# Loads issued by ScalarE, a planner that counts the DMA engines, and the last residual on GpSimd alone, in a four-layer graph network kernel

## The chip, the core and the metric

The kernel runs on one core of a Trainium2 chip. A core has a matrix engine (TensorE, PE in the profile, with its weight loads as PEld), a vector engine (VectorE, DVE), an activation engine (ScalarE, ACT), GpSimd (POOL) and a fifth sequencer, SyncE (SP), that only issues transfers here. Each of them works through its own instruction stream in order and waits for the others by semaphores. Transfers are issued by an instruction of one of these streams, and are then carried out by 16 DMA engines. The metric is the device time of one execution in microseconds (us); shorter is better.

## What is computed

For 128 graphs of 128 nodes with 256 features each, four layers run one after the other. Each normalises the features of a node, takes the ReLU, runs a graph layer, and adds the result to x:

```python
h = jnp.maximum(_layernorm(x, axis=-1), 0.0)
# layer 0: gated graph network, L = 3 steps with their own weight[i] and one common GRU cell
A = (adj != 0).astype(x.dtype)
for i in range(L):
    m = jnp.einsum('bnd,de->bne', h, weight[i])
    aggr = jnp.einsum('bst,bsd->btd', A, m)
    gi = aggr @ w_ih.T + b_ih
    gh = h @ w_hh.T + b_hh
    i_r, i_z, i_n = jnp.split(gi, 3, axis=-1)
    h_r, h_z, h_n = jnp.split(gh, 3, axis=-1)
    r, z = sigmoid(i_r + h_r), sigmoid(i_z + h_z)
    n = jnp.tanh(i_n + r * h_n)
    h = (1.0 - z) * n + z * h
x = x + h
...
# layer 1: y = sum over relations r = 1..4 of (adj == r) @ h @ weight[r], plus a bias
# layers 2 and 3: graph attention, softmax over the neighbours of e = leaky(s1_i + s2_j), then alpha @ (h W)
```

All data are float32. The adjacency matrix holds only 0 and 1, so three of the four relations of layer 1 are empty.

## The kernel before

**Tiling.** The graphs are cut into NG = 32 groups of G = 4 graphs. All buffers are preallocated: three tiles `xs` for x, five `adjs` for adjacency matrices, 24 `form`, 11 `big`, three `wide`, eight PSUM banks. A group passes through load, norm, three GRU steps (`step`), layer 1 (`neighbours`), the two attentions (`attention`, `attend`) and a store. Up to `AHEAD = 5` groups are in work at a time, so that TensorE always has products of one group while another waits.

**Three-pass products.** A float32 operand is split into parts of the type fp32r: `hi` (a rounding, line 955 or 957), `lo` (line 961) and `df`, a difference of the two (`difference`, line 470). The product then takes three passes of TensorE with a rescaling of the PSUM bank between the second and the third (`rescale`, line 1013; `scale` at line 830 in layers 1 and 2). The GRU products are line 992. In layers 1 and 2 the same splitting is used (`THIN = (1, 2)`, lines 806 to 834, product line 819), except in the last `PLAIN = 2` groups; layer 3 uses plain float32 products (line 775). Both kernels have these constants.

**Transposes.** `turn` (line 478) transposes a tile of 128x512 without TensorE: a block transpose on VectorE (line 490), a "give" that writes it to a `swap` tile in HBM (line 493), and a "take" of four transfers that reads it back in another order (line 502). After each GRU step the new h comes back this way. After the last step it is added to x (`residual`, lines 1078 to 1083), by VectorE or GpSimd as the planner finds it best.

**Loads.** `fetch` reads x in two transfers of 256 KB, twice for each group (`x0` for layer 0 and again `x1` for the residual, because there are only three `xs` tiles); `load`, `again` and the transfer at line 1095 read the adjacency matrix, again, and transposed. That is seven loads for each group, all issued by SP, in the same stream as the gives, the takes, two small transfers of each attention (lines 1151 and 1153) and the stores (line 1220).

**The order.** No engine's order is written by hand. `Plan.op` collects operations with a cost in ns, their engine (or a choice of two) and the buffers that they read and write. `Plan.order` (line 215) then plays the operations on a model of the engines while the kernel is built: it ranks each operation by the length of what follows it, by its group times `PERIOD`, and by an entry of the table `OFFSETS` (a number for each place in the code and stage of the run), and always places the operation that can start first. `LAG` and `HOP` are the delays with which one engine sees another's result. A transfer is an operation of 470 ns on SP, and its result is seen 4500 ns later (`LAG["SP"]`), changed by `late` (`GIVE`, `TAKE`, `LINE`, `SPREAD`). An operation with `port=True` does not overlap another such one on VectorE or GpSimd in the model (line 349). On the chip only the resulting order counts: every instruction waits for its semaphores, whenever the model thought that they would come.

**The branch.** The program holds two versions of most of the run, one for adjacency matrices with relations above 1. With these inputs the first is taken, and all counts below are of it.

Of the kernel before, what the change touches and what calls it, by code (L numbers as in the profile page):

```python
# [10 lines left out]
I32 = mybir.dt.int32  # L11
# [7 lines left out]
P = 128  # L19
D = 256  # L20
KC = D // P
G = 4
# [12 lines left out]
LAG = {"PE": 165, "ACT": 110, "DVE": 85, "POOL": 20, "SP": 4500, "ACTQ": 2500}  # L35
# [3 lines left out]
OWN = {"PE": 0, "ACT": 125, "DVE": 125, "POOL": 80, "SP": 2500, "ACTQ": 2500}  # L39
PERIOD = 29902  # L40
CLOSE = 7183
CLOSING = 2
SOON = -210
# [3 lines left out]
LINE, SPREAD = 0, -1000  # L47
GIVE = -400
TAKE = -2500
TENSOR = ()  # L50
BLOCK = 32
NEAR = 69
# [20 lines left out]
def seen(o, h):  # L73
    return o.late + (LAG[o.eng] + HOP[h.eng] if h.engs != (o.eng,) else OWN[o.eng])


def act(n, ptrs=0):
    return 50 + 95 * ptrs + 0.833 * n


def dve(n):
    return 68 + n / 0.96


def dma(kb):
    return 470
# [3 lines left out]
    0: (-70252, -12514, 2287, 8809, -26238, -146194, 10750, 55634, 30994, -54821, -2879, -215, -254,),  # L90
    1: (-77596, -18751, -40109, -33244, -13055, -53723, -68528, 1773, -34806, -135119, 879, -98768, 51856,
        44795, -64452, -2716,),
    2: (-95804, -20611, 70568, -66959, -6282, -38365, 6331, 7167, -87557, -120685, 144159, 0, -60172, 22200,
        253, 2907, 38047,),
    3: (-102445, -23990, 38859, 16506, -38395, -77755, 61821, 576, 58832, 37279, 38392, 48590, -137270, -161,
        -4329, 88294, -5659, -1511, -24936, -35483,),
    4: (9420, 6970, 96990, 45577, 14137, -3081, -28597, -108133, -850, -77398, -8748, -81, 24213, -39147,
        5274, -117520, -39070, 4328, 73461, 2677, -9322, 38218,),
    5: (-53063, -10484, 13614, 9709, -9223, 0, 86360, -49387, 3891, -79089, 22834, -12125, 42, -143071,
        -20815, -7001, 39402, 8197, 210921, 979, -8129, 55104, -109511, 178418, -171023, -17919, -45955,  # L100
        32785, 202299, 15929, -75290, -16189,),
    6: (-8401, 1876, 0, -2867, -17545, -54409, -177384, 6635, -4173, 16809, 64025, 1422, -41374, 3498, 7298,
        112681, -960, 0, -167733, 3047, -20901, 48681, -50794, 104147, -14530,),
    7: (2011, -43268, -7473, -2193, -13120, 17374, 10030, 24727, -8835, -59753, 29500, -32772, -10542,
        -85496, -6214, -47593, 4322, -5746, -43839, -101654, -3101, 9392, -18883,),
    10: (31340, 140410, 166041, 86764, 86271, -82403, 47762, 173067, 157481, -33091, 90840, -8460, 85813,),
    11: (-90811, -5747, -11338, -10756, 2168, -27498, -36330, -9110, 13623, -65824, 59954, -36485, 65854,
        102114, -39462, 10659,),
    12: (-88894, -2718, 120398, -47746, 16864, -33143, 17060, 25017, -58235, -111482, 170409, 89873, -65258,
        61044, 3422, 23111, 49690,),  # L110
    13: (-59071, 17894, 109447, 41927, -4268, -51312, 111328, 77067, 108356, 88471, 46360, 263340, -35253,
        23414, 79162, 211888, 10834, -10383, 74698, 67176,),
    14: (-32758, 12684, 122607, -43352, -20519, -34186, -56784, -88737, -18648, -122741, -24236, -29303,
        31876, -49287, -17477, -128202, -71886, 71670, 64769, 11212, -103569, -34527,),
    15: (-186417, -106904, -40789, -64266, -8033, -13445, 16411, -115394, -129609, -221523, -34547, -153159,
        -40482, -146129, -99541, -93701, -50044, 14115, 99121, -155460, -34394, 49772, -135635, 90451,
        -238640, -50117, -75732, -67304, 110359, -120923, -153053, -106347,),
    16: (90192, 31519, 28924, 59971, 13927, -108659, -126696, 35607, 7022, 44259, 134646, 83504, 72967,
        -71833, 139898, 214088, -4475, 66727, -178916, 46932, 84371, 67621, 13000, 119832, 93548,),
    17: (2011, -43268, -7473, -2193, -13120, 17374, 10030, 24727, -8835, -59753, 29500, -32772, -10542,  # L120
        -85496, -6214, -47593, 4322, -5746, -43839, -101654, -3101, 9392, -18883,),
    20: (-107741, -75380, -118420, -44708, -69924, -229335, -95079, 10513, -7484, 27055, -96949, -215, -254,),
    21: (-241039, -37443, -85617, -204164, -130954, -212658, -180409, -165567, -39823, -261311, -133885,
        -103620, -20641, -66103, -225402, -138454,),
    22: (-120431, -90137, 129948, -127092, 11177, -90000, -80347, -35815, -106293, -139261, 141530, -54256,
        -129233, 7860, -119111, 29072, 3576,),
    23: (-144176, -87227, -85789, 1378, -81324, -238467, -3162, -78700, 46997, -3871, 33809, 42358, -177604,
        -35904, -119077, -63937, -38348, -135903, -24936, -35483,),
    24: (-200969, -199448, -70412, -199813, -160146, -250664, -235592, -342997, -205357, -303708, -186137,
        -202706, -168399, -243146, -236370, -300082, -270699, -214705, -104544, 2677, -9322, 38218,),  # L130
    25: (-61251, -50204, -55609, -84828, -90010, 10545, -51986, -177143, -111208, -144284, 59013, -46623,
        -56779, -179794, -83802, -190091, -64080, -63359, 54466, -41363, -72589, -54011, -140205, 135055,
        -306980, -77123, -140787, 32785, 202299, 15929, -75290, -16189,),
    26: (-81589, -13318, 8156, -109205, -83353, -110277, -231535, -35494, -89897, 10694, 20288, -77730,
        -166910, -72981, -43136, 895, -48027, -102602, -242066, -114463, -91143, 43689, -72571, 104147,
        -14530,),
    27: (2011, -43268, -7473, -2193, -13120, 17374, 10030, 24727, -8835, -59753, 29500, -32772, -10542,
        -85496, -6214, -47593, 4322, -5746, -43839, -101654, -3101, 9392, -18883,),
# [19 lines left out]
class Op:  # L158
    __slots__ = ("engs", "eng", "times", "ns", "fn", "deps", "heirs", "bufs", "group", "key", "port", "rush", "late", "rank", "wait", "ready", "end", "most", "tag")
# [12 lines left out]
class Plan:  # L172
    def __init__(self):
        self.ops = []
        self.group = 0
        self.shared = True
        self.keys = 0
        self.most = 0
        self.stage, self.sites = 7, {}

    def op(self, eng, ns, fn, r=(), w=(), after=(), port=None, rush=0, late=0):

        o = Op(*((eng, ns) if isinstance(eng, tuple) else ((eng,), (ns,))), fn, self.group)
        o.port = eng == "POOL" if port is None else port
        o.rush, o.late, o.most = rush, late, self.most
        if self.shared:
            o.key = self.keys  # L190
            self.keys += 1
# [1093 lines left out]
```

## Time and profile before

| what | value |
|---|---|
| time, median of 3 runs | 2342.71 us (2341.92 to 2347.65) |
| the profiled execution | 2353.06 us, of which the profile's span is 2351.2 us |
| granted TensorE clock | 0.996 of full speed on average |
| GRU products, line 992 | 6912 matmuls of 128x512, of 12137 matmuls in all |
| differences on GpSimd, line 470 | 383 of `form` (mean 1362 ns) and 120 of `cform` (mean 1294 ns) |
| residual, line 1080 | 47 on VectorE (mean 870 ns), 13 on GpSimd (mean 1315 ns) |
| rescaling, line 1013 | 448 on ScalarE (mean 574 ns); on VectorE 128 (line 1011, mean 695 ns) |
| moved over DMA | 270.36 MB, mean 115 GB/s; nearly all of it on queue q1, that of SP |

The span is the time from the first to the last instruction that the profile saw; what is left of the execution's own time, 1.9 us, lies around it. The busy time of TensorE counts matmuls that overlap in its pipeline with modelled ends, so 97% does not mean that nothing could be gained beside the remaining 3%: the distance from start to start of two GRU matmuls in an undisturbed row is 0.229 us (11.92 us for 52 of them in the chain of waits). "Idle before" in a row is idle time of that engine alone.

### The profile page before, as it was taken

Reading aid. Unit: us, or ns where it says so; the run is one execution under the profiler, and the core shown is the slowest. Engines: PE = TensorE matmul, PEld = TensorE weight load, DVE = VectorE, ACT = ScalarE, POOL = GpSimd, SP = SyncE. Lnnn points to the kernel's source line nnn. Section 1 sums busy time; section 2 is a strip of 40 time slices with the busy share of each in tenths; the row PEclk is TensorE's granted clock in tenths of the full one; section 3 lists DMA queues with packets and bytes.
Section 4 is the critical chain, followed back from the end, with each engine's and each line's share of the span. In section 5 each row is a group of like instructions: output and inputs, shape, how many; then the busy total and the mean of one; then the engine's idle time right before and its main releaser. Section 6 shows DMA issues by size and latency. Waiting matters only on the chain.

```text
span 2351.2 us, 39064 instructions
## 1 busy us (share of the span) xinstructions
PE 2291.9 (97%) x12137; PEld 1947.2 (83%) x12137; DVE 1978.2 (84%) x5405; ACT 1582.0 (67%) x3272; POOL 912.4 (39%) x729
## 2 busy tenths in 40 slices
PE   7999999999999999999999999999999999999997
PEld 6788888888888888888888888888888888788885
DVE  7858888888888888888888888888888888888887
ACT  6566676766676666666666766666766666666665
POOL 2334334443334443334343334343334343344421
PEclk9999999999999999999999999999999999999999
DMA  8535445555445455455455455455554555545431
GB/s 249 143 83 110 96 90 124 117 128 116 102 110 125 111 133 113 100 117 117 114 126 118 107 115 115 114 129 116 108 115 112 118 122 109 128 103 118 105 77 43
DMA packets 951273, 270.36 MB, mean 115 GB/s; under 512 B 677008, under 2 KB 939280, under 8 KB 951056
## 3 DMA queue, kind: packets, MB, share of 16 engines
q1 hardware_dynamic: 949968, 266.72, 50.0%
q8 instruction: 99, 1.62, 0.3%
q14 instruction: 118, 0.97, 0.2%
q10 hardware_dynamic: 1088, 1.05, 0.1%
HBM read 168.96 MB, written 98.69 MB: 114 GB/s over the span
## 4 chain that ended last, share of the span: by engine, by line
PE 64%; DVE 14%; DMA 10%; ACT 6%; SPq 4%; issue 3%; DVEq 0%; POOL 0%; ACTq 0%
PE bank L992 40%; PE bank L819 7%; PE bank L765 6%; PE bank L974 5%; PE bank L775 5%; DMA swap<-big 4%; SPq L502 4%; DMA big<-swap 3%; DVE junk L1119 3%; DVE form L961 2%; DMA wide<-swap 2%; ACT big L743 1%; DVE wide L1042 1%; DVE wide L1045 1%; DVE big L490 1%
## 5 line engine op out<-in xcount | busy, mean ns | idle before, releaser
L992 PE MATMUL bank<-form,wh_s 128*128 128x512 f32 x3456 | 953.4, 396 | 8.7 <-ACT bank L1005 4.6
L992 PE MATMUL bank<-form,wi_s 128*128 128x512 f32 x3456 | 944.0, 393 | 1.6 <-ACT bank L1013 0.9
L470 POOL TENSOR_TENSOR form<-form,form 128x512 fp32r<-128x512 f32 x383 | 517.7, 1362 | 800.4 <-DVE form L961 565.0
L992 PEld LDWEIGHTS bank<-form,wi_s 128*128 128x128 f32 x3456 | 644.1, 188 | 143.6 <-ACT bank L1013 3.1
L992 PEld LDWEIGHTS bank<-form,wh_s 128*128 128x128 f32 x3456 | 631.8, 188 | 151.5 <-ACT bank L1005 15.8
L1013 ACT ACTIVATE bank<-bank 128x512 f32<-128x512 f32 x448 | 255.4, 574 | 325.7 <-PE bank L992 324.4
L722 POOL TENSOR_TENSOR small<-small,nhalf 128x4 f32<-128x4 f32 (+2 forms) x140 | 142.2, 1020 | 408.8 <-DVE small L720 338.9
L1119 DVE CUSTOM_DVE_ANT_0 junk<-big,ub 128x256 bf16<-128x256 f32 x512 | 244.5, 478 | 14.2 <-ACT big L743 0.5
L743 ACT ACTIVATE big<-xs,small 128x256 f32<-128x256 f32 x384 | 200.1, 590 | 21.6 <-DVE small L726 12.2
L696 DVE BATCH_NORM_STATS2 small<-xs 128x6 f32<-128x256 f32 x512 | 190.0, 415 | 7.3 <-DMA xs<-in_x_dram 6.0
L470 POOL TENSOR_TENSOR cform<-cform,cform 128x512 fp32r<-128x512 f32 x120 | 155.2, 1294 | 96.2 <-DVE cform L811 83.0
L490 DVE STREAM_TRANSPOSE big<-wide 128x512 f32<-128x512 f32 x252 | 173.1, 697 | 4.0 <-ACT wide L743 2.3
L1035 DVE SCALAR_TENSOR_TENSOR bank<-big,bank 128x512 f32<-128x512 f32 x192 | 131.9, 690 | 48.5 <-PE bank L992 35.9
L955 ACT ACTIVATE form<-wide 128x512 fp32r<-128x512 f32 x179 | 109.2, 626 | 83.7 <-DMA wide<-swap 43.4
L1179 ACT ACTIVATE big<-big,small 128x128 f32<-128x128 f32 x256 | 99.8, 392 | 70.0 <-DVE small L1173 69.7
L1023 ACT ACTIVATE bank<-bank,b_rz 128x512 f32<-128x512 f32 x192 | 123.4, 655 | 34.0 <-PE bank L992 30.1
L1210 DVE SCALAR_TENSOR_TENSOR xs<-bank,small,xs 128x256 f32<-128x256 f32 x256 | 118.4, 475 | 31.6 <-PE bank L775 23.0
L1042 DVE TENSOR_TENSOR wide<-wide,bank 128x512 f32<-128x512 f32 x192 | 126.9, 682 | 21.4 <-ACT bank L1040 21.1
L765 PE MATMUL bank<-big,big 128*128 128x128 f32 x1024 | 130.7, 277 | 11.9 <-DVE wide L1045 7.1
L1023 ACT ACTIVATE big<-bank,b_rz 128x512 f32<-128x512 f32 x192 | 130.1, 681 | 16.3 <-PE bank L992 12.1
L765 PEld LDWEIGHTS bank<-big,big 128*128 128x128 f32 x1024 | 123.1, 192 | 19.4 <-DVE wide L1045 9.9
L974 PE MATMUL bank<-adjs,big 128*128 128x128 f32 x1024 | 131.2, 276 | 6.4 <-DMA big<-swap 5.1
(105 smaller groups left out, 3297.5 us busy)
## 6 DMA issues: line engine op xcount, KB each, us to landing
swap<-big SPq DMA_DIRECT2D x312, 256.0 KB, 2.5
big<-swap SPq DMA_DIRECT2D x992, 64.0 KB, 2.3
xs<-in_x_dram SPq DMA_DIRECT2D x128, 256.0 KB, 3.1
adjs<-in_adj_dram SPq DMA_DIRECT2D x64, 256.0 KB, 3.4
wide<-swap SPq DMA_DIRECT2D x128, 128.0 KB, 3.6
big<-line SPq DMA_DIRECT2D x60, 256.0 KB, 3.9
out_dram<-xs SPq DMA_DIRECT2D x30, 512.0 KB, 3.1
big<-in_adj_dram SPq DMA_DIRECT2D x32, 256.0 KB, 4.0
```

The lines of the kernel that those rows point to most:

```text
L470: (nc.gpsimd if eng == "POOL" else nc.vector).tensor_tensor(at(df), at(lo).bitcast(F32), at(hi).bitcast(F32), ALU.subtract)
L490: nc.vector.transpose(part.t, src())
L696: op("DVE", dve(D), lambda g=g: nc.vector.bn_stats(s.t[:, ST + 6 * g : ST + 6 * g + 6], xt.t[:, g, :]), r=[(xt, {g})], w=[(s, {("mv", g)})])
L743: nc.scalar.activation(place(g), xt.t[:, g, :].rearrange("p (k m) -> p k m", k=KC), AF.Relu, bias=s.t[:, MR + g : MR + g + 1], scale=s.t[: ...
L765: nc.tensor.matmul(ps.t[:, (len(gs) * k + j) * P : (len(gs) * k + j + 1) * P], hs[g // 2].t[:, (g % 2) * D + k * P : (g % 2) * D + (k + 1) ...
L819: nc.tensor.matmul(po.t[:, j * D : (j + 1) * D], fs[f].t[:, (len(gs) * k + j) * P : (len(gs) * k + j + 1) * P], w.t[:, f, k, :], start=(st ...
L974: nc.tensor.matmul(pg.t[:, g * P : (g + 1) * P], of()[:, g * P : (g + 1) * P], flags(m0)[:, g * P : (g + 1) * P], start=True, stop=True,)
L992: nc.tensor.matmul(ps.t, w.t[(slice(None), *row, j, k, slice(c * P, (c + 1) * P))], b.t, start=(start and x == 0), stop=(x == len(terms) - ...
L1013: nc.scalar.mul(ps.t, ps.t, by)
L1023: op("ACT", act(T, 1), lambda: nc.scalar.activation(to.t, ps.t, AF.Tanh, bias=b_rz.t[:, c : c + 1], scale=0.5), r=[b_rz, *([ps] if kept el ...
L1042: op("DVE", dve(T), lambda c=c, ps=ps: nc.vector.tensor_tensor(hT.t[:, c, :], hT.t[:, c, :], ps.t, ALU.subtract), r=[ps], w=[(hT, {c})])
L1119: nc.vector.tensor_tensor_reduce(out=junk.t, in0=part, in1=ub[i].t[:, v, :], op0=ALU.mult, op1=ALU.add, scale=1.0, scalar=0.0, accum_out=s ...
```

## The change

1. **The seven loads of each group go from SP's stream to ScalarE's.** A new function `arrive` issues them with `nc.scalar.dma_start` when `QUEUE` is "ACT". The weights, gives, takes, stores and the small transfers stay where they were.
2. **The planner counts the DMA engines.** A transfer gets a length `moves`. In `place` a running time `engines` is pushed on by each transfer, and the result is seen at its end plus `LAND` = 1400 ns plus `late`, in place of a fixed 4500 ns; `GIVE` and `TAKE` are 0, and a load on ScalarE's queue has `late` = 4700. An issue costs 530 ns.
3. **GpSimd and VectorE may overlap by `EASE` = 400 ns in the planner's model of their port,** and a few costs of operations are a little larger (`act`, `dve`, the attention terms 880 for 850).
4. **The residual of the last step runs on GpSimd alone.**
5. **All of `OFFSETS`, and `PERIOD`, `CLOSE`, `SOON` and `NEAR`, have new values,** so the order of every engine is new.

```diff
-LAG = {"PE": 165, "ACT": 110, "DVE": 85, "POOL": 20, "SP": 4500, "ACTQ": 2500}
+LAG = {"PE": 165, "ACT": 110, "DVE": 85, "POOL": 20, "SP": 0, "ACTQ": 0}
...
-OWN = {"PE": 0, "ACT": 125, "DVE": 125, "POOL": 80, "SP": 2500, "ACTQ": 2500}
-PERIOD = 29902
-CLOSE = 7183
+OWN = {"PE": 0, "ACT": 125, "DVE": 125, "POOL": 80, "SP": 0, "ACTQ": 0}
+PERIOD = 30728
+CLOSE = 21788
...
-SOON = -210
+SOON = -2537
...
-LINE, SPREAD = 0, -1000
-GIVE = -400
-TAKE = -2500
+LAND = 1400
+LINE, SPREAD = 1300, 100
+GIVE = 0
+TAKE = 0
...
+ISSUE = 530
+EASE = 400
+LANDING = 4700
+ARRIVAL = 2300
+QUEUE = "ACT"
...
-NEAR = 69
+NEAR = 41
...
 def seen(o, h):
-    return o.late + (LAG[o.eng] + HOP[h.eng] if h.engs != (o.eng,) else OWN[o.eng])
+    return (o.late + LAND + o.dma if o.dma is not None else 0) + (LAG[o.eng] + HOP[h.eng] if h.engs != (o.eng,) else OWN[o.eng])
...
+            o.seen = end
+            if o.dma is not None:
+                n = P // BLOCK if o.ns == ISSUE * P // BLOCK else 1
+                engines = max(max(engines, end - (n - 1) * ISSUE) + o.dma, end + o.dma / n)
+                o.seen = engines + LAND + o.late
             if o.port and eng != "ACT":
-                port = max(port, end)
+                port = max(port, end - (EASE if eng == "POOL" else 0))
...
+        def arrive(dst, src, w, after=()):
+            on_act = QUEUE == "ACT"
+            op(QUEUE, dma(256), lambda: (nc.scalar if on_act else nc.sync).dma_start(out=dst(), in_=src), w=w,
+               after=after, late=LANDING if on_act else ARRIVAL, moves=800)
+
         def fetch(gi, name, after=()):
             xt = Buf(xs, f"{name}{gi}")
             for g2 in range(G // 2):
-                op("SP", dma(256), lambda g2=g2: nc.sync.dma_start(
-                    out=xt.t[:, 2 * g2 : 2 * g2 + 2, :],
-                    in_=x[ds(gi * G + 2 * g2, 2)].rearrange("g n d -> n g d")),
-                   w=[(xt, {2 * g2, 2 * g2 + 1})], after=after)
+                arrive(lambda g2=g2: xt.t[:, 2 * g2 : 2 * g2 + 2, :],
+                       x[ds(gi * G + 2 * g2, 2)].rearrange("g n d -> n g d"), [(xt, {2 * g2, 2 * g2 + 1})], after)
...
                 for k, h in enumerate(hs_new if i == L - 1 else ()):
-                    def residual(eng, k=k, h=h):
+                    def residual(k=k, h=h):
                         part = xt.t[:, :, k * P : (k + 1) * P]
-                        (nc.gpsimd if eng == "POOL" else nc.vector).tensor_tensor(
-                            part, part, h.t.rearrange("p (g d) -> p g d", g=G), ALU.add)
-
-                    op(("DVE", "POOL"), (dve(T), 1250), residual, r=[h], w=[(xt, set(range(G)))], port=True)
+                        nc.gpsimd.tensor_tensor(part, part, h.t.rearrange("p (g d) -> p g d", g=G), ALU.add)
+
+                    op("POOL", 1250, residual, r=[h], w=[(xt, set(range(G)))], port=True)
```

## The prediction

> **What bounds the kernel now.** I read the busy shares, then windows of the run, then who made TensorE wait, then the waits on the engines that the change touches.
>
> ```profile
> PE 2291.9 (97%) x12137; PEld 1947.2 (83%) x12137; DVE 1978.2 (84%) x5405; ACT 1582.0 (67%) x3272; POOL 912.4 (39%) x729
> ```
>
> TensorE is busy for all but 59 us. Windows (length, then busy PE, PEld, DVE, ACT, POOL) say where those are:
>
> ```profile
> 0.00:60.00 60.00, 44.82 (x181) 36.36 (x182) 43.11 (x116) 37.42 (x101) 14.68 (x18) 0.91 0.88 248
> ...
> 1000.00:1400.00 400.00, 398.32 (x2140) 341.33 (x2139) 345.32 (x929) 272.61 (x551) 161.27 (x126) 1.00 0.51 116
> ...
> 2300.00:2351.20 51.20, 36.33 (x187) 28.73 (x185) 38.62 (x222) 27.61 (x84) 11.39 (x18) 0.91 0.17 49
> ```
>
> 15.2 us lie in the first 60 and 14.9 in the last 51; between them only 29 us are idle in 2240. VectorE, at 345.3 of 400, is the next engine. What held TensorE up (total, times, longest):
>
> ```profile
> PE bank L765 <- DVE wide L1045: 7.1, 12, 1.5
> PE bank L598 <- DMA big<-in_wihT_dram: 6.3, 1, 6.3
> PE bank L765 <- ACT big L743: 5.3, 1, 5.3
> PE bank L974 <- DMA big<-swap: 5.1, 8, 1.5
> ...
> PE bank L992 <- ACT bank L1005: 4.6, 7, 1.0
> PE bank L765 <- DMA big<-swap: 3.9, 6, 1.6
> ```
>
> So it is TensorE's own work plus many small stalls. Counted over the executed branch, TensorE has the same 10271 instructions in both programs, three-pass products included: their part of the change's name is no change here. Between start and end only stalls can be gained. If every idle microsecond in the middle went (29) and the ends stayed, the profiled execution would take about 2324 us; that is nearly the floor.
>
> **1. The residual leaves VectorE.** It waits in order for a take to land:
>
> ```profile
> DVE xs L1080 <- DMA big<-swap: 66.5, 45, 3.3
> ```
>
> 47 adds of 870 ns are 41 us of VectorE's work, and 69.6 us of its idle time precede them. What stands behind waits too: at 342.6 us VectorE has waited 2.1 us for the take, and TensorE's next GRU products start 0.34 us late, released by ScalarE's L1005. All seven stalls "L992 <- L1005" (4.6 us) come within 6 us of such a residual; with smaller ones of the same cause I take **-6 us** (ends: 0, if the new order has its own such waits, and -12). On GpSimd the 47 adds cost 47 x 1.315 = 62 us, and the wait stands there before differences and the norm's power. GpSimd has 1439 idle us. The new order also takes 95 differences (63 `form`, 32 `cform`) off it.
>
> **2. VectorE and ScalarE get other work.** Counts of both orders times the rows: VectorE gains 96 x 0.67 (differences; one row has it at 674 ns) + 28 x 0.68 + 40 x 0.68 + 26 x 0.42 (roundings) = 121 us, and loses 41 (residual) + 76 x 0.695 = 53 (rescalings): net +27 us, from 84% to 85%. ScalarE gains 76 x 0.574 = 44 us and loses 28 x 0.595 + 40 x 0.597 + 26 x 0.626 = 57. All this lies beside TensorE's work. A difference on VectorE takes half of GpSimd's 1362 ns, which shortens the way to the third pass; 27 us more on the second-fullest engine leaves less room. I take **0** (ends -10 and +27, all of it uncovered).
>
> **3. The loads leave SP.** There are 224. SP waited with them at its head:
>
> ```profile
> SPq L513 <- ACT wide L743: 120.6, 54, 8.9
> SPq L513 <- DMA out_dram<-xs: 69.9, 25, 4.4
> ```
>
> 190 us in which gives and takes queued behind could not be issued. The Trainium skill speaks against an effect: in "DMA: Bandwidth & Descriptors", section "Issuing engines are not separate DMA queues", all issuers' transfers interleave on the same 16 DMA engines, and a second issuer saves only the sequencer's time. By that rule I would count 224 x 0.47 us of SP's time, which bounds nothing: 0. The rows show more than issue time, a wait in the queue, with late takes as 9.0 us of TensorE's stalls (L974 and L765 above). I take the rows, less one: **-8 us** (ends 0 and -9).
>
> **4. ScalarE issues them.** One issue takes it about 0.5 us (three in 1.57 us at the start), so 224 take 112 us, and ScalarE goes from 67% to about 72%. Behind each issue stand tanh, exponentials and rescalings that free PSUM banks. In the new order 16 loads stand right before a rescaling, and 43 right before a gate's tanh. Moreover every transfer of the program waits until the one issued eight before it has landed (eight semaphores in turn), whichever queue it is on. In steady state, for one of seven loads in a group, the second half of x0, the eighth before is a take only about 2.8 us of TensorE work earlier; a take needs up to four issues and 2.3 us, so ScalarE may stand 0 to 1.5 us there. ScalarE has about 23 idle us in a group's 71, and the order leaves over 3 us of TensorE work, by the matmuls in between, before a GRU product that depends on it. I take **0** in the steady part (ends 0 and +36; see the second rival).
>
> **5. The start.** The eight-transfer limit is visible before:
>
> ```profile
> 0.73 0.48 ACTq L542 DMA_DIRECT2D big<-in_w0T_dram  x1
> ...
> 2.24 4.30 SPq L513 DMA_DIRECT2D xs<-in_x_dram  x4
> 2.84 1.28 ACT L580 ACT_TABLE_LOAD   x1 [2.84 <-issue]
> ```
>
> SP issues four loads and ScalarE four; then SP stands until first ones land, while ScalarE is free from 2.8 us and splits its first weights at 8.38. In the new program 13 transfers (nine loads of x and adjacency, four of weights) stand before ScalarE's first activation. The last of them is the 23rd transfer of all, and before the 23rd was issued at 14.40 us. So ScalarE begins some 5 us later. Weights `whh` come earlier in exchange (first on SP), and ScalarE has some 14 idle us between 8 and 60 to catch up. I take **+4 us** (ends 0 and +6).
>
> **6. The end.** After the last GRU product both orders have the same 35.3 us of TensorE work by the planner's costs, in 62 operations, and no loads: **0** (ends -4 and +4). The planner's new accounting costs nothing at run time; what it does is in the order.
>
> **Sum:** -6 + 0 - 8 + 0 + 4 + 0 = -10 us on the profiled 2353.06 (span 2351.2 plus 1.9), 2343.1, a ratio of 0.9958. On the median of 2342.71 that is **2333 us**, some 0.4% faster.
>
> **The rivals.**
> - *No change.* TensorE is full, the late takes and the VectorE waits were covered but for 4.6 + 9 us, and a new order has new places with thin cover, as the old one has (L765 behind L1045 recurs in many groups). Gains and the start cancel: 2343 us. For it: 398.3 busy of 400 in the best window leaves little. Against: other windows are worse (394.8 from 600 to 1000).
> - *Slower: ScalarE is held by its loads.* Place: load issues and their waits in ScalarE's stream, ahead of rescalings. Price: 7 x 0.5 + about 1.3 of waiting = 4.8 us in a group. It decides once ScalarE is so late that TensorE has used up its cover; with a quarter reaching TensorE, 1.2 us x 30 groups = 36, plus 4, less the 14 gained: +26 us, 2379 profiled, **2369 us**. For it: the order was planned without the eight-transfer limit, and a load that waits for a store or a reader now blocks ScalarE and not SP. Against: a third of ScalarE is idle.
> - *Slower: VectorE becomes the bound.* 27 us more, uncovered, less part 3 and plus part 5: 27 - 8 + 4 = +23 us, **2366 us**. Against: 85% is not full, and the residual's waits go.
>
> **Chances.** The forecast 0.45 (own range 2310 to 2336), no change 0.23, ScalarE held 0.22, VectorE 0.10. A measurement of this kernel tells 0.3% (7 us) from nothing: faster 0.45, same 0.23, slower 0.32. The range, with the unknown ends in it: low 2308 (the cited gains at their far ends, -12 - 10 - 9 - 4 = -35), high 2372 for the two slower cases.
>
> **What would show it.** Right: L1080 gone from VectorE's waits, no L513 row among SP's, fewer stalls of L974 and L765 for takes, ScalarE's first activation near 13 us, TensorE's middle windows above 99%. Wrong: rows in which ScalarE's DMA issues wait long and L992 waits for L1013 or L1005 in every group; VectorE above 88% in the middle windows; GpSimd's residual wait delaying L992 through L470.

## The result, and the profile after

The changed kernel takes 2500.53 us (median of 4, 2498.53 to 2504.74), beside 2343.34 us for the kernel before on the same chip (2341.92 to 2347.65): a ratio of 1.0668 [1.065, 1.0685], 157 us slower, where 2333 us and a gain of 0.4% were forecast. In the new program the lines stand 14 to 16 lower: the GRU products are L1008, their rescaling on ScalarE L1029, the aggregation L990, the residual L1096, the loads L527.

The same three views of the changed kernel's profile as were read before: busy time and share, windows, and who made TensorE wait (total, times, longest).

```profile
PE 2335.9 (93%) x12137; PEld 1959.4 (78%) x12137; DVE 2119.0 (85%) x5472; ACT 1569.4 (63%) x3253; POOL 855.8 (34%) x681
```

```profile
0.00:60.00 60.00, 35.30 (x152) 28.76 (x153) 40.60 (x110) 32.53 (x90) 10.61 (x14) 1.00 0.79 230
1000.00:1400.00 400.00, 377.33 (x1973) 316.12 (x1972) 346.38 (x882) 253.72 (x523) 140.59 (x109) 0.99 0.48 109
2440.00:2502.90 62.90, 48.43 (x225) 38.72 (x224) 44.34 (x244) 31.00 (x97) 10.76 (x18) 0.83 0.14 40
```

```profile
PE bank L990 <- DMA big<-swap: 51.7, 23, 3.8
PE bank L835 <- ACT bank L846: 34.3, 30, 1.8
PE bank L1008 <- ACT bank L1029: 16.8, 19, 1.8
```

TensorE has the same 12137 matmuls. It idles 167.0 us of the span (2502.9 less 2335.9) in place of 59.3, and its busy time, whose ends are modelled, is 44.0 us longer, at a granted clock of 0.986 in place of 0.996. The loss is not at the ends: the window in the middle has 22.7 us of idle TensorE in 400, where before it had 1.7. And it is not that another engine is full: VectorE is at 346.4 of 400 (345.3 before), ScalarE at 253.7 (272.6). All work more slowly together.

What is new among the waits of the other engines, in three answers for ScalarE, VectorE and GpSimd:

```profile
ACT adjs L870 <- DMA adjs<-in_adjT_dram: 68.0, 30, 3.2
ACT adjs L865 <- DMA adjs<-in_adj_dram: 58.2, 32, 4.3
...
DVE small L712 <- DMA xs<-in_x_dram: 66.0, 50, 4.9
...
DVE adjs L948 <- DMA adjs<-in_adj_dram: 21.5, 25, 1.0
...
POOL xs L1096 <- DMA big<-swap: 156.5, 23, 10.1
```

ScalarE stands 126.2 us at loads of adjacency and VectorE 87.5 at loads. (L865, L870 and L948 convert a loaded adjacency matrix from int32, L712 takes the statistics of a loaded x; they are the first users of their loads.) Before, the same answers have 2.1 and 7.7 us, mostly these:

```profile
ACT adjs L849 <- DMA adjs<-in_adj_dram: 1.9, 2, 1.0
...
DVE small L696 <- DMA xs<-in_x_dram: 6.0, 3, 4.3
```

One such place, in the timeline of ScalarE (start, duration, instruction; in brackets the idle time before it):

```profile
1206.14 0.66 ACT L1021 ACTIVATE bank<-bank,b_hn 128x512 f32<-128x512 f32 x1
1207.00 0.60 ACT L822 ACTIVATE cform<-bank 128x512 fp32r<-128x512 f32 x1 [0.20 <-PE bank L781]
1207.01 0.37 ACTq L527 DMA_DIRECT2D adjs<-in_adjT_dram  x1
1209.83 0.62 ACT L870 CAST adjs<-adjs 128x512 f32<-128x512 int32 x1 [2.23 <-DMA adjs<-in_adjT_dram]
1210.35 0.66 ACT L1021 ACTIVATE bank<-bank,b_hn 128x512 f32<-128x512 f32 x1
```

ScalarE issues the load at 1207.01 and the very next instruction of its stream uses it, at 1209.83; the rescalings and gates behind that wait as well. In the changed order this is so for 56 of the 64 adjacency loads that ScalarE converts. Why does the planner put the user there? In `Plan.op` of the changed kernel, line 197, only an operation whose engine is called SP or ACTQ is a transfer:

```
o.dma = (300 if moves is None else moves) if o.engs[0] in ("SP", "ACTQ") else None
```

`arrive` makes the load an operation of "ACT". So its `dma` is None, `place` lets its result be seen at the end of the issue, and `late`, `LAND` and `moves` are never used: the 4700 ns of `LANDING`, listed above as part of the change, are dead text. On the chip a load lands 2.9 to 4.2 us after its issue (medians; last column of the page's transfers; 2.9 is that of adjT):

```profile
swap<-big SPq DMA_DIRECT2D x312, 256.0 KB, 2.8
big<-swap SPq DMA_DIRECT2D x992, 64.0 KB, 2.4
xs<-in_x_dram ACTq DMA_DIRECT2D x128, 256.0 KB, 4.2
adjs<-in_adj_dram ACTq DMA_DIRECT2D x64, 256.0 KB, 3.0
```

In the old order a median of 5.0 to 9.2 us of TensorE work, by the planner's costs, stand between a load and its first user, in the new one 0.9 to 1.4. (The second x, x1, had 23.8 and has 4.6.)

### The profile page after: what moved, and what is told of

Same layout as the page of the kernel before. It is cut to its first block, busy times and chain, and to the rows that moved or that the text cites. A ratio compares the mean times of both kernels' runs of the same rounds, so it can differ in the third digit from the quotient of the medians.

```text
span 2502.9 us, 39059 instructions
## 1 busy us (share of the span) xinstructions
PE 2335.9 (93%) x12137; PEld 1959.4 (78%) x12137; DVE 2119.0 (85%) x5472; ACT 1569.4 (63%) x3253; POOL 855.8 (34%) x681
## 5 line engine op out<-in xcount | busy, mean ns | idle before, releaser
L1008 PE MATMUL bank<-form,wh_s 128*128 128x512 f32 x3456 | 977.2, 404 | 6.2 <-DVE wide L1064 2.7
L1008 PE MATMUL bank<-form,wi_s 128*128 128x512 f32 x3456 | 957.9, 397 | 20.0 <-ACT bank L1029 16.8
L1008 PEld LDWEIGHTS bank<-form,wi_s 128*128 128x128 f32 x3456 | 644.7, 190 | 180.5 <-ACT bank L1029 37.7
L1008 PEld LDWEIGHTS bank<-form,wh_s 128*128 128x128 f32 x3456 | 634.0, 190 | 134.4 <-DVE wide L1064 6.1
L485 POOL TENSOR_TENSOR form<-form,form 128x512 fp32r<-128x512 f32 x320 | 427.4, 1340 | 878.4 <-DVE form L977 691.3
L1029 ACT ACTIVATE bank<-bank 128x512 f32<-128x512 f32 x528 | 300.3, 576 | 365.8 <-PE bank L1008 363.0
L1133 DVE CUSTOM_DVE_ANT_0 junk<-big,ub 128x256 bf16<-128x256 f32 x512 | 292.4, 571 | 13.3 <-ACT big L759 2.9
L712 DVE BATCH_NORM_STATS2 small<-xs 128x6 f32<-128x256 f32 x512 | 195.5, 413 | 73.7 <-DMA xs<-in_x_dram 66.0
L990 PE MATMUL bank<-adjs,big 128*128 128x128 f32 x1024 | 143.8, 286 | 59.4 <-DMA big<-swap 51.7
L990 PEld LDWEIGHTS bank<-adjs,big 128*128 128x128 f32 x1024 | 135.6, 200 | 76.8 <-issue 55.2
L485 POOL TENSOR_TENSOR cform<-cform,cform 128x512 fp32r<-128x512 f32 x88 | 114.8, 1305 | 165.2 <-DVE cform L827 146.3
L1096 POOL TENSOR_TENSOR xs<-xs,big 128x512 f32<-128x512 f32 x60 | 79.6, 1327 | 258.4 <-DMA big<-swap 156.5
L977 DVE SCALAR_TENSOR_TENSOR form<-form,wide 128x512 fp32r<-128x512 f32 x192 | 141.2, 749 | 1.5 <-ACT form L971 1.2
L835 PE MATMUL bank<-wa,cform 128*128 128x256 f32 x720 | 110.0, 288 | 33.0 <-ACT bank L846 31.7
```

The costliest lines, as they stand in the source:

```text
L485: (nc.gpsimd if eng == "POOL" else nc.vector).tensor_tensor(at(df), at(lo).bitcast(F32), at(hi).bitcast(F32), ALU.subtract)
L712: op("DVE", dve(D), lambda g=g: nc.vector.bn_stats(s.t[:, ST + 6 * g : ST + 6 * g + 6], xt.t[:, g, :]), r=[(xt, {g})], w=[(s, {("mv", g)})])
L977: op("DVE", dve(T), lambda: nc.vector.scalar_tensor_tensor(lo.t, f(hi), -1 / UNIT, src(), ALU.mult, ALU.add), r=[dep, hi, token], w=[lo], ...
L990: nc.tensor.matmul(pg.t[:, g * P : (g + 1) * P], of()[:, g * P : (g + 1) * P], flags(m0)[:, g * P : (g + 1) * P], start=True, stop=True,)
L1008: nc.tensor.matmul(ps.t, w.t[(slice(None), *row, j, k, slice(c * P, (c + 1) * P))], b.t, start=(start and x == 0), stop=(x == len(terms) - ...
L1029: nc.scalar.mul(ps.t, ps.t, by)
```

## The experiments

**First: where is the load's cost?** Theory 1: the landing that the order doesn't see. Theory 2: ScalarE's time for issues and the limit of eight transfers. Theory 3: VectorE and GpSimd beside each other, and the residual. Four kernels, against 2344.08 us of before:

```
a_seen:    line 197: ... if o.engs[0] in ("SP", "ACTQ") or moves is not None else None   (planned anew)
a_later:   the changed order; loads up to 7 us of TensorE work earlier, conversions L865, L870, L948 as much later
a_spissue: the changed order; (nc.scalar if on_act else nc.sync).dma_start -> nc.sync.dma_start
b_act:     the order of before; its seven loads: nc.sync.dma_start -> nc.scalar.dma_start
```

> The changed kernel, with one line of the planner altered: a load on ScalarE's queue counts as a transfer (length 800, then LAND and LANDING), where the change took its result as seen at the end of the issue. Theory 1 (the planner does not know when these loads land, so their users stand right behind them and hold ScalarE and VectorE): the waits of L865, L870, L948 and L712 for loads (214 us together) fall below 40 us, and the time comes to 2345 to 2400 us (ratio to before 1.00 to 1.025). Theory 2 (ScalarE's issuing, with the limit of eight transfers, is what costs): above 1.05. Theory 3 (planned overlap of VectorE and GpSimd on their port, and the residual on GpSimd): above 1.04, VectorE's L1133 still near 571 ns.

> The changed kernel's order as it is, but each load moved up to 7 us of TensorE work ahead where its buffer is free, and the conversion of each adjacency matrix (L865, L870, L948 of the changed kernel) moved up to 7 us of TensorE work back; TensorE's order does not change. Theory 1: ScalarE's 126 us of waits for loads go nearly to 0, the time falls by at least a third of the loss, to a ratio of 1.02 to 1.045. Theories 2 and 3: stays within 0.7% of 1.067.

> The changed kernel's order as it is, the loads issued by SyncE at the same place of the program instead of ScalarE. Theory 1: the users still stand right behind the loads, no better, a ratio of 1.06 to 1.10 (SyncE is late more often than ScalarE). Theory 2: most of the loss goes, below 1.035. Theory 3: within 0.7% of 1.067.

> The kernel before, its order as it is (at least 5 us of TensorE work between a load and its first user), the seven loads of each group issued by ScalarE at the same places of the program. Theory 1: little, a ratio of 0.99 to 1.01. Theory 2: 1.03 or more, with load issues waiting on ScalarE and L992 waiting for L1013 and L1005. Theory 3: 1.00.

Measured: a_seen 2539.77 us, 1.0837 [1.0819, 1.0855]; a_later 2493.14, 1.0646 [1.0629, 1.0664]; a_spissue 2529.75, 1.0792 [1.0763, 1.0821]; b_act 2364.83, 1.0093 [1.0076, 1.0109].

Only b_act answers cleanly: the issue by ScalarE costs 21 us where the order leaves room for the landing, so theory 2 is 0.9% and not 6.7% (4.0 of the 21 us lie in the first 60, at the start); and back on SP (a_spissue) the changed order is worse still. The other two were badly made. a_seen has the waits for loads gone, but the table `OFFSETS` had been fitted to the other account: by the planner's own account, which before and after say 2289 and 2286 us, this plan takes 2409. (The account is arithmetic at build time, no measurement; the chip's distance from it is what I compare below.) In a_later the loads were moved up to right behind the operations that free their tiles, so ScalarE stood at the issue instead (125 semaphore waits at 224 issues, the longest 6.3 us, for 43 and 2.9 us in the changed kernel), and TensorE with it:

```profile
PE bank L1033 <- ACT bank L1046: 66.1, 36, 3.6
PE bank L1033 <- ACT bank L1054: 28.5, 41, 2.3
```

Those are the GRU products (L1033 there) behind ScalarE's rescalings.

**Second: VectorE beside GpSimd.** The rows looked suspicious: the attention terms (L1119 before, L1133 after) went from 478 to 571 ns each,

```profile
L1119 DVE CUSTOM_DVE_ANT_0 junk<-big,ub 128x256 bf16<-128x256 f32 x512 | 244.5, 478 | 14.2 <-ACT big L743 0.5
```

```profile
L1133 DVE CUSTOM_DVE_ANT_0 junk<-big,ub 128x256 bf16<-128x256 f32 x512 | 292.4, 571 | 13.3 <-ACT big L759 2.9
```

and a difference on VectorE from 674 ns (there is only one before) to 1011 for `form` and 1237 for `cform`. With smaller ones that is about 110 us more busy VectorE than the moved work explains. Four kernels, in a session in which the kernel before took 2365.03 us:

```
a_diffpool:    the changed order; all differences nc.gpsimd.tensor_tensor
b_diffdve:     the order of before; 64 form and 32 cform differences nc.vector.tensor_tensor
a_ease0:       EASE = 400 -> EASE = 0     (planned anew)
a_seen_ease0:  EASE = 0 and a_seen's line 197     (planned anew)
```

> The changed kernel's order as it is, but the 96 differences that it gives to VectorE (104 us there, mean 1011 and 1237 ns) are made by GpSimd at the same place. Theory A (VectorE's time sets the period: in the kernel before, the changed one and all four variants so far it is busy 83 to 85% of the span, and its work grew by 141 us, 27 by other operations and about 112 by the same operations taking longer beside GpSimd): VectorE's busy time falls to about 2010 us and the time to 2370 to 2410 us (ratio 1.01 to 1.03). Theory B (an order without reserve, so that each late result is passed on, whatever the engine): a later third form makes it no better, 1.055 to 1.08.

> The kernel before, its order as it is, with the same number of differences (64 of form, 32 of cform, spread evenly) made by VectorE instead of GpSimd. Theory A: VectorE's work rises by 65 us or more, the time by about as much over 0.84: 2410 to 2430 us (ratio 1.03 to 1.04). Theory B: the reserve of this order takes it up, below 1.012.

> The changed kernel planned with EASE = 0: no planned overlap of VectorE and GpSimd on their port. The table OFFSETS was made for another model, so the new order is worse by the planner's own account, which ends at 2437 us (before 2288, changed kernel 2284, measured 55 and 216 us above these). What counts here is the distance of the measurement to that account. If the port is what the account misses: VectorE's L1133 falls from 571 to below 500 ns, L485 on VectorE to below 800, and the distance from 216 to about 216 - 112 = 104 us or less (2500 to 2540 us). If the port is not it: L1133 stays, and the distance is 180 us or more (2620 and above).

> EASE = 0, and a load on ScalarE's queue counts as a transfer in the planner. The planner's own account ends at 2472 us; the kernel with the second alone had 2407 and was measured at 2540, a distance of 133 against 216. If the unseen landing and the port are the whole miss: a distance of 30 to 75 us (2500 to 2545 us), as the kernel before has 55. If something else is missed as well: above 100 us (2575 and more).

Measured: a_diffpool 2537.34 us, 1.074 [1.0711, 1.077]; b_diffdve 2370.74, 1.0019 [1.0006, 1.0033]; a_ease0 2645.14, 1.1171 [1.1139, 1.1203]; a_seen_ease0 2591.45, 1.0942 [1.0912, 1.0971].

VectorE with 96 more differences, 685 and 673 ns each there, costs the old order 0.2%: its load does not set the period. Taken away from VectorE in the changed order (a_diffpool), they leave the terms at 572 ns and gain nothing. Planned without overlap, the terms are back at 472 ns in the trace of a_ease0, and yet nothing is gained; but the accounts of the last two (2438 and about 2470) are worse too, so they show little else.

**Third: lateness alone, taken away and added.** From here on an order was kept and only loads or their users were moved, or `OFFSETS` was searched again.

```
a_users:    the changed order; only the conversions L865, L870, L948 later, by some 7 us of TensorE work
b_late:     the order of before, loads on SP; loads of x0, adj, adjT later, to 0.9 to 2.3 us before their users
b_late_act: the same, with nc.scalar.dma_start for the seven loads
```

> The changed kernel with its own order, in which only the conversions of adjacency tiles (two on ScalarE, one on VectorE) are moved later, by some 7 us of TensorE work each; their results are needed 35 us of TensorE work later or more, and no load is moved. Between the issue of an adjacency load and its first user stand then 8 to 9 us of TensorE work in place of 1.4. The loads of x keep 0.9. Theory 1 (the order takes a load for landed when it is issued, so ScalarE and VectorE stand at loads that are under way): the waits of ScalarE for the two adjacency loads (126 us together) and of VectorE's conversion (22 us) go, and with them some half of what was lost: 2390 to 2440 us, ratio 1.02 to 1.04, VectorE's 66 us for x staying. Theory 2 (ScalarE's time for issuing, and the places in line) and theory 3 (VectorE beside GpSimd): no load is issued elsewhere and no operation changes its neighbours on GpSimd, so 2485 to 2515, ratio 1.06 to 1.073.

> The kernel before with its own order and all its loads on SP, in which only the loads of the first x, of adj and of adjT are moved later, until some 0.9 to 2.3 us of TensorE work stand between a load and its first user (as in the changed kernel, in place of 5 to 9). This adds the suspected cost alone: nothing is issued by ScalarE, nothing moves between VectorE and GpSimd. Theory 1: ScalarE and VectorE stand at each of the six loads of a group for 1 to 3 us, the chain is 3 to 6 us longer in each of 24 groups: 2410 to 2490 us, ratio 1.03 to 1.065. Theories 2 and 3: 2340 to 2355 us, ratio 1.00 to 1.005, since SP is not busy and what it issues instead comes a little earlier.

> The run with late loads in the order of before, with those loads and the second x issued by ScalarE in place of SP: the whole of the suspected cause on the kernel before, without the change's VectorE and GpSimd part. Loads issued early by ScalarE cost 0.9% in an earlier run. Theory 1: the two add up, 20 us more than the same loads on SP or somewhat less, as a load behind ScalarE's own work is issued later still: ratio 1.04 to 1.08. Theory 2 alone: 1.005 to 1.015 as in the earlier run. Theory 3: 1.00 to 1.015.

Measured, against 2344.15: a_users 2473.79, 1.0553 [1.0534, 1.0572]; b_late 2525.57, 1.0778 [1.0758, 1.0798]; b_late_act 2394.86, 1.0223 [1.0203, 1.0243]. a_users gave back 27 us, less than half of the least that theory 1 said. In its trace ScalarE's waits for adjacency are gone, but VectorE stands 87.6 us at loads of x in place of 66.0, and TensorE 35.5 us at ScalarE's rescalings in place of 16.8: part of the waiting moved.

Late loads cost the old order 181 us on SP but, over b_act, only 30 on ScalarE. The loads land equally fast in both (medians 3.0 to 3.3 us from the issue), yet ScalarE stands much longer at them. First b_late, then b_late_act:

```profile
ACT adjs L871 <- DMA adjs<-in_adjT_dram: 126.8, 31, 7.4
ACT adjs L866 <- DMA adjs<-in_adj_dram: 85.2, 26, 5.6
```

```profile
ACT adjs L866 <- DMA adjs<-in_adj_dram: 33.6, 30, 4.1
ACT adjs L871 <- DMA adjs<-in_adjT_dram: 12.6, 8, 3.1
```

So on SP it is the issue that comes late. When ScalarE is free for the conversion, the load was issued 4.4 us (adjT) and 2.3 us (adj) ago in b_late_act; in b_late it is only issued then, 0.6 and 0.1 us after (medians of 32; in the changed kernel 0.6 and 1.1 us before). One such place, in the timelines of SP and ScalarE of b_late:

```profile
1057.84 4.41 SPq L519 DMA_DIRECT2D big<-swap  x8
1062.35 0.43 SPq L1112 DMA_DIRECT2D adjs<-in_adjT_dram  x1
...
1067.29 0.62 ACT L871 CAST adjs<-adjs 128x512 f32<-128x512 int32 x1 [5.86 <-DMA adjs<-in_adjT_dram]
```

ScalarE is free at 1061.43, while SP is still issuing the eight transfers of two takes ahead of the load. So lateness is a real cost, and theory 1 as it stood, a stall for each load added up, was too simple.

**Fourth: all waiting for loads removed, and all parts without the new order.** In a_aside, from the seventh group on, the loads are issued as ever but into two tiles that nobody reads; conversions read a constant tile, and x keeps what its tile held, so these kernels leave out the use of the loaded data in 26 of the 32 groups. In b_all the old order is kept operation by operation, with loads on ScalarE, the residual on GpSimd and 96 differences on VectorE.

```
+ if plan.group >= 6:
+     dst = away                     # a_aside; a_aside_adj: for adjacency only
...
- op(("DVE", "POOL"), (dve(T), 1250), residual, ...        issued by nc.gpsimd in every case (b_all)
```

> The changed kernel with its own order. From the seventh group on, the loads of x and of the adjacency tiles are issued by ScalarE at the same places and with the same sizes, but into two tiles that nothing reads; the three conversions of adjacency read a constant tile in place of the loaded one, and x keeps what its buffer held. So nobody waits for a load, and no load waits for its buffer: its issue and its bytes stay, the change's split between VectorE and GpSimd stays. (What the kernel computes is not the reference's in those groups.) Theory 1, that the users of loads stand right behind them because the order takes a load for landed when it is issued: on the critical way of the changed kernel's trace I count 137 us at loads; 26 of 32 groups lose them, some 100 to 140 us less: 2360 to 2405 us, ratio 1.007 to 1.026. Theory 3, VectorE's operations beside GpSimd's, with the waits for loads lying beside other stalls: 2440 to 2490 us, ratio 1.04 to 1.06. Theory 2, ScalarE's time for issuing: above 2470, as its issues all stay.

> The same, but only the adjacency loads go into the unread tiles; those of x stay as they are, with VectorE's statistics and GpSimd's residual behind them. Moving the conversions away from the loads brought 26 us. Theory 1: adjacency is half of what stands at loads, so 2425 to 2470 us, ratio 1.035 to 1.053, between the changed kernel and the run with all loads set aside; the rest of that run's gain belongs to x. Theory 3: within 30 us of the changed kernel, and of the run with all set aside too.

> The order of the kernel before, kept operation by operation, with three parts of the change put on it: ScalarE issues the loads at the places where SP did, the last h is added to x by GpSimd alone, and VectorE makes 64 and 32 of the differences. The planner and its order are left out of it. Singly, loads on ScalarE cost 0.9% and the differences 0.2%; the residual was not run alone in this order. Theory 1 (the order is the cause, not the parts): the parts add up to 1.01 to 1.025, 2367 to 2403 us. Theory 3 (the parts are the cause, VectorE beside GpSimd above all): 1.04 to 1.07.

> The run with all three parts on the order of before, in which the loads of the first x, of adj and of adjT are moved later as in the late run on ScalarE, to 0.9 to 2.3 us of TensorE work ahead of their first users. Lateness alone, on ScalarE, cost 1.3% over the same loads issued early. Theory 1 as it stood (lateness is most of the 6.7%): 1.045 to 1.07, near the changed kernel. If lateness in an order with room between its other steps costs no more than 1.3%: 1.023 to 1.04, and then the tightness of the changed order is part of the cause.

Measured, against 2342.69: a_aside 2456.21 us, 1.0478 [1.0457, 1.05]; a_aside_adj 2467.9, 1.0537 [1.0519, 1.0554]; b_all 2389.59, 1.0203 [1.0186, 1.022]; b_all_late 2414.74, 1.0317 [1.0293, 1.034].

b_all splits the loss: the parts cost 47 us in an order made without them, so **some 110 us belong to the new order** (with the rescalings and roundings that it gives to another engine). Late loads on top of the parts add 25 us (b_all_late). ScalarE and VectorE stand 97 us at loads there, less than half of the 214 of the changed kernel, so the lateness of that kernel was not fully copied. a_aside says that the waits for loads are 44 us of the loss (in 26 of 32 groups), less than half of the 100 to 140 expected; a_aside_adj, that 33 of these are adjacency. So 88 us more of such waits (97, from 9 in b_all) cost the old order 25 us, and 174 us fewer (39 are left in a_aside) give the new one 44 back: about a quarter of a wait reaches the time in both, and for loads the new order is hardly less forgiving than the old. What took the place of the loads stands in TensorE's waits of a_aside, where L1006 is the aggregation:

```profile
PE bank L1006 <- DMA big<-swap: 63.1, 27, 3.4
```

With the loads out of the way TensorE waits longer for takes than in the changed kernel (51.7): the transposes' way through HBM was just as late.

**Fifth: takes set aside, and two searched orders.** a_aside_swap is a_aside with the takes written, from the seventh group on, to tiles in HBM that nobody reads; their readers use what stands in their own tiles. t_seen is a_seen with `OFFSETS` searched until its account fell from 2409 to 2325 us. t_margin also allows a give 2.0 us more, and was searched to 2323, so the two differ in where the order has room, not in how long they say they are. They also differ in what each search chose otherwise (88 and 70 differences on VectorE).

```
a_aside_swap:  + to = afar[n][hop[0] % 4] if there else dst()
t_seen:        line 197 as in a_seen; OFFSETS searched
t_margin:      line 197 as in a_seen; GIVE = 0 -> 2000; LANDING = 4700 -> 2300; OFFSETS searched
```

> The run with all loads set aside (2456 us), in which, from the seventh group on, the takes of the transposes too are written to tiles in HBM that nobody reads, and their readers use what stands in their own tiles. So neither loads nor takes are waited for; their issues, gives and transfers stay, as does the split between the engines. (What it computes is not the reference's in those groups.) In the trace of that run TensorE stood 63 us at takes, and on its critical way 62 us are at them. If the rest of the loss is the missing allowance of the swap transfers (4.1 us for a give in the old account, 2.0 in the new one, 2.2 to 3.5 measured): some 26 of 32 groups lose these waits, 2390 to 2420 us, ratio 1.02 to 1.033, what the parts cost alone in the order of before. If it is VectorE beside GpSimd, the takes' waits are replaced by others: 2435 to 2460 us.

> The planner of the change with the one-line mend (a load on ScalarE counts as a transfer), and with OFFSETS searched anew by the planner's own account until that said 2325 us (2409 without the search; the changed kernel's account says 2286, that of before 2289). The chip stood 131 us above the account in the mended run without a search, 215 in the changed kernel, 54 before. If the waits for loads were all that the account missed, the distance is near that of before: 2380 to 2400 us, ratio 1.015 to 1.025. If the account also gives gives and takes too little time, the distance stays at 110 to 140: 2435 to 2465 us, ratio 1.04 to 1.052.

> The same as the mended and searched run, but the account allows 2.0 us more for each give (4.0 us, about as the planner of before did), and 4.5 us in place of 6.9 for a load; searched anew to 2323 us, so that both have the same account. Overlap of GpSimd and VectorE stays as in the change. If the allowance of the swap transfers is what else the order lacks: the distance falls to 60 to 90 us, 2385 to 2413 us, 40 to 60 us below the mended run. If VectorE beside GpSimd is: within 15 us of the mended run.

Measured, against 2344.81: a_aside_swap 2367.92 us, 1.0093 [1.0066, 1.012]; t_seen 2435.91, 1.0389 [1.0362, 1.0417]; t_margin 2395.63, 1.0215 [1.0189, 1.024].

One thing in those expectations is wrong: the old account did not give a give 4.1 us. A take stands on SP behind its give, so `OWN["SP"]` counts and not `LAG["SP"]`: 2500 - 400 = 2100 ns. The allowance for a give hardly changed (2.1 to 2.0 us); for a load it fell from 4.5 us to nothing. What t_margin adds is room that neither order's account asked for.

The window 1000 to 1400 us of a_aside_swap:

```profile
1000.00:1400.00 400.00, 398.30 (x2135) 338.52 (x2134) 366.07 (x943) 270.90 (x553) 156.23 (x121) 1.00 0.51 117
```

TensorE is as full as before the change, with VectorE at 366.1 of 400 and its terms still at 572 ns: **VectorE beside GpSimd does not by itself cost the time** (whether it lengthens the other waits is not shown). The loads set aside gave 44 us and the takes another 88, together more than the order's 110: some of the takes' waits belong to the parts, as that of the residual on GpSimd, which stands 217.7 us at takes in a_aside and 26.9 in this run. Then SP's waits, first of t_seen, then of t_margin, where L519 is the take that stands at the head of SP until its give has landed:

```profile
SPq L519 <- DMA swap<-big: 317.7, 171, 4.0
```

```profile
SPq L519 <- DMA swap<-big: 37.7, 52, 2.0
```

That wait alone is not the cost. The kernel before has as much of it, with TensorE at 398.3 of 400:

```profile
SPq L502 <- DMA swap<-big: 279.1, 176, 4.3
```

What counts is who needs the take by then. TensorE's waits for takes at the aggregation, first of t_seen, then of t_margin:

```profile
PE bank L992 <- DMA big<-swap: 21.1, 22, 2.4
```

```profile
PE bank L992 <- DMA big<-swap: 3.2, 5, 1.6
```

VectorE's norm behind GpSimd's residual, which waits for takes, stood 55.7 us and stands 10.1. TensorE has 396.5 of 400 us in the middle window in place of 385.7:

```profile
1000.00:1400.00 400.00, 385.72 (x2064) 328.26 (x2063) 352.00 (x890) 268.04 (x544) 152.89 (x119) 1.00 0.51 114
```

```profile
1000.00:1400.00 400.00, 396.54 (x2138) 337.49 (x2137) 355.82 (x918) 270.35 (x551) 162.75 (x127) 1.00 0.51 115
```

Each of the two is one order of many. How far two orders of the same account lie apart by chance was not measured, so the 40 us between them are not all shown to come from the room for gives. None of the kernels beats the one before.

## Why the prediction was wrong

The loss in one line: 157 us = 47 for the parts (b_all) + 110 for the order. Counting the landing and searching again (t_seen) takes off 65, the order with room for the gives another 40, and t_margin then lies 6 us from b_all: at about before plus the parts. The chip's distance from the planner's account tells the same: 54 us before, 215 in the changed kernel, 111 in t_seen, 73 in t_margin.

**The step that failed** is the last sentence of part 6: "The planner's new accounting costs nothing at run time; what it does is in the order." The order was never read for it. Part 4 looked at what stands behind each issue ("16 loads stand right before a rescaling, and 43 right before a gate's tanh") and at the limit of eight, but not at where the load's own user stands, nor at whether a load on "ACT" still is a transfer in line 197. Both could be read in the code and in the two orders without a run. What the runs showed in its place: the parts of the change, which the sum had at -10 us, cost 47, and the order, which it had at nothing, costs 110. In that order the users of loads stand right behind them, so that ScalarE and VectorE stand 214 us at loads, of which 44 reach the time (a_aside), and TensorE waits 54.9 us for takes in place of 9.0; without the waits for both, the changed kernel takes 2367.92 us (a_aside_swap).

Point by point:
- *1, the residual (-6).* L1080 did leave VectorE's waits, and the stalls counted for it (L992 behind L1005, 4.6 us) shrank, to 0.6 us in b_all and 1.3 in the changed kernel. But the wait only moved: GpSimd stands 156.5 us at takes, and in b_all, with the old order, VectorE's next norm stands behind GpSimd's residual (0.3 us before; 5.7 in the changed kernel, where it is hardly passed on to VectorE):

```profile
DVE small L703 <- POOL xs L1087: 76.3, 26, 5.0
```

  In b_all TensorE's waits for the new h (L765 behind L1045 before) rose from 7.1 to 20.7 us. b_all less b_act and b_diffdve leaves 2.03 - 0.93 - 0.19 = 0.9%, about +21 us, for the residual and what the three do together; it was not run alone, and the three runs come from different sessions. As far as b_all shows it, the sign was wrong: the wait was kept and 445 ns an add (1.315 for 0.870 us) were put on its way.
- *2, the re-split (0).* Right for the differences (b_diffdve: 0.2%). That VectorE's operations would become about 110 us longer was not foreseen; in a_aside_swap it did not keep TensorE from 398.3 of 400.
- *3, loads leave SP (-8).* L513 left SP's waits, as said, yet TensorE's waits for takes went from 9.0 us to 54.9. In b_act, with the old order, the aggregation's waits for takes rose from 5.1 to 15.1 us, and SP stood 670.9 us at gives whose input VectorE had not made yet, in place of 371.5: the time that the loads left free went there. The rule weighed there (the Trainium skill, "DMA: Bandwidth & Descriptors", "Issuing engines are not separate DMA queues") gave 0 and was nearer to b_act's +21 us than the rows that I took: they show a wait at SP's head, and not that its end was needed earlier.
- *4, ScalarE issues them (0, ends 0 and +36).* In the old order +21 us: within the ends.
- *5, the start (+4, ends 0 and +6).* TensorE's idle time in the first 60 us grew by 44.82 - 35.30 = 9.5 us; ScalarE's first activation is at 17.8 us and not near 13. In b_act, which moves the loads alone, it grew by the forecast 4.0 us (first activation at 15.4); the rest came with the new order.
- *6, the end (0).* Right: 14.5 us idle in the last 62.9 (13.7 in the last 51.2), 14.9 in the last 51.2 before.

The rival "ScalarE is held by its loads" had the engine right, and of its sign "DMA issues wait long" little came: it is the instruction behind the issue that waits. It said +26 us, as it counted issues and a place in line, not a landing of 3 us in front of rescalings.

What stays open is how the order's 110 us divide between loads and takes. Taken out of the same order they are 44 and then 88; in orders planned again 65 and then 40. They are not independent. And the takes of the kernel before were not set aside as a control; TensorE stood only 9.0 us at them.

## What to carry to other kernels

When a transfer is moved to another queue, look in that engine's stream for its first user and for the work in between, and compare it with the landing in the trace; an issue in a compute engine's stream is cheap (0.37 us for most loads here), a user right behind it holds that engine for the rest of the landing. When a kernel's order comes from a model, find what each changed operation counts as in it, and leave room for how much transfers vary (gives landed after 2.3 to 7.4 us in t_seen): of two orders that the model called equally long, the one with 2 us more for each give was 40 us faster. A long wait at the head of a transfer queue is no cost in itself; look for who needs what stands behind it. To price the parts of such a change, put them on the old order one by one before looking at the new one.

## What the hardware showed besides

- Beside GpSimd's operations VectorE's took longer: 478 to 571 ns for the terms in the order that was planned to overlap them by 400 ns, 472 in a_ease0, planned apart; 685 and 673 ns (b_diffdve) to 1011 and 1237 for differences. A VectorE 91.5% busy (366.07 of 400) still let TensorE run at 398.3 of 400.
- The granted clock was 0.996 over the run before, 0.986 after and 0.961 in a_ease0, the longest. But it does not follow TensorE's idle time alone: it was 0.991 in b_late, with 177 us idle, and in the first 60 us it was 0.91 before, with 15.2 us idle, and 1.00 after, with 24.7. What sets it stays open.
- The same loads landed differently in the changed kernel: those of x later (median 4.2 us, 3.1 before), those of adjacency sooner (3.0 for 3.4, 2.9 for 3.6), at a lower mean rate (108 GB/s, 115 before).
